# Reordering the attention of the last four batches: value corrections ahead of the key and query corrections, odd chunks' keys turned one chunk early, and the choice of tokens in two steps

## The chip, the cores and the metric

The kernel runs on one core of a Trainium2 chip. The metric is device time in microseconds (us) from one launch. All data are float32. Five engines work side by side from queues of their own: TensorE (PE in the profile; PEld are its weight loads), VectorE (DVE), ScalarE (ACT), GpSimd (POOL) and SyncE (SP), which here only issues DMAs. TensorE writes to PSUM, the others copy results from there to SBUF.

## The reference

A layer of the macaron kind on x of shape 8 x 1024 x 512: half of an expert FFN, attention, half of the same expert FFN, each on the layer-normed x and added to it.

```python
x = x + 0.5 * ffn(layernorm(x), gate_w, gate_b, w1, w2)
x = x + attn(layernorm(x), Wq, bq, Wk, bk, Wv, bv, Wo, bo)
x = x + 0.5 * ffn(layernorm(x), gate_w, gate_b, w1, w2)

# attn, 16 heads of 32, linear and causal
q, k = exp(x @ Wq.T + bq), exp(x @ Wk.T + bk); v = x @ Wv.T + bv
kv = cumsum(k[..., :, None] * v[..., None, :]); k1 = cumsum(k)
out = (q @ kv) / sum(q * k1); out = out @ Wo.T + bo

# ffn: 32 experts, each chooses 8 tokens of each batch
probs = softmax(x @ gate_w.T + gate_b, over tokens)
vals, idx = top_k(probs.T, 8)
merged = sum over the 8 of x[idx] * vals                # one row per expert
o = gelu(merged @ w1 + b1) @ w2 + b2
out[idx] += o * vals
```

## The kernel before

The kernel has four stages, which show in the trace: the choice for the first FFN (to about 145 us), the first FFN (to about 815 us), attention (to about 1930 us) and the second FFN. Both FFNs stream 256 blocks of 2 MB of expert weights through TensorE.

The first FFN is bound by that stream, so a generator `speculate` runs beside it and projects the centred x of batches 4 to 7 with Wq, Wk and Wv. Queries, keys and values of each pair of chunks are stored in DRAM (`ahead_d`). They are projections of x before the FFN's output is added. In attention such a batch is only corrected: the FFN's output for a batch is a sum of 32 expert rows, so the correction is a matmul of 32 rows with the projected expert rows (`oW` for q and k, `oWv` for v), scaled by the tokens' 1/sigma.

Attention takes the 8 batches in turn, each in 8 chunks of 128 tokens. Two chunks make a unit. Batches 0 to 3 are projected in place (`project`), batches 4 to 7 come from `project_rest`, a generator with four steps:

- A (L627 to L658): ask for the next unit's `pre`, add the output bias to x (GpSimd), broadcast 1/sigma with two matmuls (`ps_rs`), copy it (`rsb`), multiply it into the chosen probabilities (`pmr`) and into the loaded projections `pre` (GpSimd, two of 128x1024)
- B (L660 to L682): 16 matmuls `ps_qk` (in fours of 32 rows) into the PSUM tiles `sp0` and `sp1`; VectorE adds them to `pre` (`un`, L676, two of 128x1024); ScalarE takes eight exponentials (L679)
- C (L684 to L706): two matmuls `ps_v`; VectorE scales and adds (`va`, L697, two)
- D (L707 to L709): running sums of the keys (`sum_keys`, four scans, L720) and their product with the queries (`times_keys`, GpSimd, L731)

One chunk c of batch b, in the loop of `attention`: `scores` (32 matmuls into `sp0` and `sp1`, masked by VectorE at L788 and by ScalarE and GpSimd at L793 and L795 into `am`), in even chunks `denominators` and step A, then `turn_keys` (four transposes `ps_kt`, copied to `kc` by ScalarE), `project_out` of the chunk before (`ps_o`, L891, with an add and the statistics on VectorE), `spread_denominators` (`ps_rr`), and `attend` (`ps_n`, scaled to `at` at L862, and the running state `ps_kv`). Beside these run two more generators. `begin` adds the FFN's output to the next batch's x (`ps_sc`, `scatter_two`, two VectorE adds and their statistics), four steps and a square root at the end of the fourth. `route` makes the second FFN's choice of the batch before: `ps_rsT`; `ps_rs` with the logits `lg` (L400); `choose` (L404: eight largest values, their indices, the others marked, exponential, product); `ps_pmT`; `ps_m`; `ps_mT`. One step is taken in each chunk.

In the code before, a unit is advanced so, where `rest` says that the unit being prepared is one of batches 4 to 7: A in the even chunk, B behind `attend` of the even chunk, then at the head of the odd chunk `turn_keys`, C and a step of `route`, and only then that chunk's `scores`; D behind `project_out` of the odd chunk, after a step of `begin`.

The pool of PSUM tiles `mm` has three banks, shared by every `ps_` tile named here apart from `sp0`, `sp1` (two banks each, used by `scores`, `ps_qk` and `ps_rr` in turn) and `ps_kv`. Within an engine a scheduler orders the instructions from the program's order and readiness as it is built; on the chip each engine follows that order.

Of the kernel before, what the change touches and what calls it, by code (L numbers as in the profile page):

```python
# [8 lines left out]
F32 = mybir.dt.float32  # L9
AF = mybir.ActivationFunctionType  # L10
ALU = mybir.AluOpType
# [9 lines left out]
def kernel(  # L21
# [382 lines left out]
    def choose(t, lg, rows, g, name, listed=False, el=None):  # L404


        top = t.p2.tile([P, 8], F32, tag="top", name=f"top_{name}")
        nc.vector.max(top[rows, :], lg[rows, :])
        pinned = el is not None
        sm = t.p2.tile([P, 3], F32, tag="sm", name=f"sm_{name}")  # L410
        nc.vector.tensor_scalar_mul(sm[rows, 0:1], top[rows, 0:1], -1.0)
        rest = pm[:, g, :]
        nc.vector.match_replace(rest[rows, :], top[rows, :], lg[rows, :], -1.0e30)
        if listed and not pinned:
            nc.vector.max_index(chosen_idx[rows, g, :], top[rows, :], lg[rows, :])
        el = el if pinned else lg
        nc.scalar.activation(
            el[rows, :], lg[rows, :], AF.Exp, bias=sm[rows, 0:1], accum_out=sm[rows, 1:2]
        )
        kept = nc.vector.scalar_tensor_tensor(  # L420
            rest[rows, :], rest[rows, :], -0.9e30, el[rows, :], ALU.is_lt, ALU.mult
        )
        if pinned:
            tc.keep_in_program_order(kept)
        nc.vector.reciprocal(sm[rows, 2:3], sm[rows, 1:2])
        if pinned:
            return rest, sm[rows, 2:3], top
        return rest, sm[rows, 2:3]

    def gather_four(t, xs, rs4, chosen, r, g):  # L430

# [48 lines left out]
    def route(t, s, b, el=None):  # L480

        g = b // 4
        own = slice(32 * (b % 4), 32 * (b % 4) + E)
        rows = own
        xt = s["xt", b][0]
        mv = s["mv", b]
        lg = t.p1.tile([P, S], F32, tag="lg", name=f"lg_{b}")
        sd = t.small.tile([P, NCH], F32, tag="sd", name=f"sd_g{b}")  # L490
        rs = t.small.tile([P, NCH], F32, tag="rs", name=f"rs_g{b}")
        at = 0
        for k in (NCH,) if el is None else (4, 2, 1, 1):
            cols = slice(at, at + k)
            nc.scalar.activation(sd[:, cols], mv[:, cols, 1], AF.Sqrt, bias=eps_t)
            if el is not None and at + k == NCH:

                junk = t.small.tile([P, 1], F32, tag="junk", name="junk")
                tc.keep_in_program_order(nc.scalar.activation(junk, eps_t, AF.Exp))
            nc.vector.reciprocal(rs[:, cols], sd[:, cols])  # L500
            for _ in gate_scale(t, s, b, lg, rs, at, k):
                if el is None:
                    yield
            at += k
            if at < NCH:
                yield
        if el is None:
            yield
        chosen, r, *top = choose(t, lg, rows, g, f"b{b}", True, el)
        diag = t.p2.tile([P, E], F32, tag="diag", name=f"diag_{b}")  # L510
        scaled = nc.vector.tensor_scalar_mul(diag[rows, :], ident[rows, rows], r)
        if el is not None:
            tc.keep_in_program_order(scaled)
            tc.keep_in_program_order(
                nc.vector.max_index(chosen_idx[rows, g, :], top[0][rows, :], lg[rows, :])
            )
        if el is None:
            yield

        pmT = t.p1.tile([P, NCH, E], F32, tag="pmT", name=f"pmT_{b}")  # L520
        ps = t.mm.tile([P, NCH, E], F32, tag="mm", name=f"ps_pmT_{b}")
        for c in range(NCH):
            nc.tensor.matmul(
                ps[:, c, :],
                lhsT=chosen[rows, c * P : (c + 1) * P],
                rhs=diag[rows, :],
                start=True,
                stop=True,
            )
# [32 lines left out]
        if el is None:  # L562
            yield
        ps = t.mm.tile([P, NDC, E], F32, tag="mm", name=f"ps_mT_{b}")
        for dc in range(NDC):
            nc.tensor.matmul(
                ps[:, dc, :], lhsT=m[:, dc * P : (dc + 1) * P], rhs=isum, start=True, stop=True
            )
        nc.vector.tensor_copy(mT[:, :, :, b], ps)
        if el is None:  # L570
            yield
# [51 lines left out]
    def project_rest(t, s, b, u):  # L623
# [33 lines left out]
            load_ahead(t, s, *divmod(b * (NCH // U) + u + 1, NCH // U))  # L657
        yield  # L658

        qkT = open_unit(t, s, b, u)  # L660
        sp = [
            t.sc.tile([P, 2, 2, UT], F32, tag=f"sp{h}", name=f"ps_qk{h}_{b}_{u}") for h in range(2)
# [14 lines left out]
        for n, bias in ((1, bk_sb), (0, bq_sb)):  # L677
            for oc in range(NDC):
                nc.scalar.activation(  # L679
                    qkT[:, oc, n, :], qkT[:, oc, n, :], AF.Exp, bias=bias[:, oc : oc + 1]  # L680
                )
        yield  # L682

        ps = [t.mm.tile([P, D], F32, tag="mm", name=f"ps_v_{b}_{u * U + i}") for i in range(U)]  # L684
        for i in range(U):
            r = slice(E * ((b + i) % 4), E * ((b + i) % 4 + 1))
            nc.tensor.matmul(
                ps[i],
                lhsT=pmr[r, i * P : (i + 1) * P],
                rhs=s["oWv", i][r, :],  # L690
                start=True,
                stop=True,
            )
        for i in range(U):
            c = u * U + i
            va = t.a2.tile([P, D], F32, tag="va", bufs=3, name=f"va_{b}_{c}")
            nc.vector.scalar_tensor_tensor(  # L697
                va,
                pre[:, (2 * NDC + i * 2) * UT : (2 * NDC + i * 2 + 2) * UT],
                rs[:, c : c + 1],  # L700
                ps[i],
                ALU.mult,
                ALU.add,
            )
            s["va", b, c] = va
        yield  # L706
        sum_keys(t, s, b, u)  # L707
        times_keys(t, s, b, u)
# [241 lines left out]
    def attention(t, early, preload):  # L950
# [44 lines left out]
        for _ in begun:  # L995
            pass
        last = None
        for b in range(B):
            for c in range(NCH):
                if c == 0:  # L1000
# [22 lines left out]
                if b == B - 1 and c == NCH - 2:  # L1023
# [4 lines left out]
                    el = end.enter_context(tc.tile_pool(name="el", bufs=1, side="right")).tile(  # L1028
                        [P, S], F32, name="el"
                    )  # L1030
                    gate = route(t, s, b, el)
                if rest and c % U:
                    turn_keys(t, s, b, c)
                    next(ahead)
                    next(gate, None)
                scores(t, s, b, c)
                if c % U == 0:
                    denominators(t, s, b, c // U)
# [23 lines left out]
                    values(t, s, b, c)  # L1062
                if not (rest and c % U):
                    turn_keys(t, s, b, c)
                if last is not None:
                    project_out(t, s, *last)
                    if c == 0:
                        for h in range(2):
                            store_x(out, s["xt", b - 1][0], b - 1, h)
                        gate_sums(t, s, b - 1, range(NCH // 2, NCH))  # L1070
                        gate = route(t, s, b - 1)
                    if c == NCH // 2:
                        gate_sums(t, s, b, range(c))
                    if b == B - 1 and c == NCH - 2:
                        gate_sums(t, s, b, range(NCH // 2, c))
                    if b == B - 1 and c == NCH // 2:
                        store_x(out, s["xt", b][0], b, 0)
                if c % U == 0:
                    spread_denominators(t, s, b, c // U)
                else:  # L1080
                    if rest and c > 1:
                        next(begun, None)
                    next(ahead, None)
                if not (rest and c % U):
                    next(gate, None)
                if (b, c) == (0, 1):
                    outputs_turned(t, s, 0)
                attend(t, s, b, c)
                if rest and c % U == 0:
                    next(ahead)  # L1090
                last = (b, c)
        gate_sums(t, s, B - 1, range(NCH - 2, NCH - 1))
# [576 lines left out]
```

## Time and profile before

| what | value |
|---|---|
| median of 3 runs | 2604.76 us (2601.95 to 2608.11) |
| profiled execution | 2606.22 us, span of its core 2604.5 us |
| mean granted TensorE clock | 0.915 |
| busy: TensorE, VectorE, ScalarE, GpSimd | 2190.8, 862.3, 500.4, 376.6 us |
| chain that ended last | TensorE 50%, issue 23%, DMA 16%, VectorE 5% |
| attention, batches 0 to 3 (830 to 1498 us) | TensorE busy 653.97 of 668 us, clock 0.99 |
| batch 4 (1518.4 to 1623.9 us) | TensorE busy 98.19 of 105.5 us, clock 0.92, VectorE 77.75 |
| batch 5 (1623.9 to 1730 us) | TensorE busy 99.45 of 106.1 us, clock 0.90, VectorE 77.23 |
| batch 6 (1730 to 1836 us) | TensorE busy 98.65 of 106 us, clock 0.92, VectorE 78.19 |
| second FFN (1900 to 2604 us) | TensorE busy 426.7 of 704 us, DMA share 0.93 |

A row of the timeline gives start, length, engine, source line, operation, output<-inputs, shape and count; in square brackets the idle time before it and what released it. Float32 matmuls are counted twice or more in the profile[...]. The busy time of a matmul at half clock is longer than at full clock, so busy time and the clock belong together. The profiled execution is 1.5 us above the median.

### The profile page before, as it was taken

The numbers are of one execution on the slowest core, as the hardware profiler recorded it, in microseconds if no ns is written. First come the engines' busy times: TensorE is split into PE (matmuls) and PEld (weight loads), VectorE is DVE, ScalarE is ACT, GpSimd is POOL, SyncE is SP. The second block draws the span as 40 slices with busy tenths as digits, with TensorE's granted clock in tenths as the row PEclk, the third lists the DMA queues.
The fourth block names the chain that finished last, engine by engine and source line by source line (L and its number), as shares of the span: only waits on it lengthen the run. The fifth ranks groups of instructions, "written<-read, shape, count | busy, mean of one in ns | idle before, by whom it ended". The sixth has DMA issues, their size and how long they took to land.

```text
span 2604.5 us, 41783 instructions
## 1 busy us (share of the span) xinstructions
PE 2190.8 (84%) x18679; PEld 1153.6 (44%) x18679; DVE 862.3 (33%) x1495; ACT 500.4 (19%) x965; POOL 376.6 (14%) x345
## 2 busy tenths in 40 slices
PE   8799999898986999999999989999986565555555
PEld 5354545444533666666666655555551111101111
DVE  6411111111102443444534466777750000100002
ACT  6310000000000322222223243343430000000000
POOL 0000000000000212111122145545324000000002
PEclk9999999999998999999999989989888878777788
DMA  7799999999996000010100233333159999999995
GB/s 276 305 426 427 427 427 427 426 427 428 427 429 255 1 18 1 21 50 20 52 9 19 79 110 124 106 113 109 68 210 389 425 427 428 428 428 428 428 427 239
DMA packets 95635, 668.22 MB, mean 257 GB/s; under 512 B 18254, under 2 KB 22606, under 8 KB 58592
## 3 DMA queue, kind: packets, MB, share of 16 engines
q1 hardware_dynamic: 73952, 621.71, 58.1%
q10 hardware_dynamic: 18432, 35.66, 3.5%
q0 software_dynamic: 3072, 8.19, 0.8%
q8 instruction: 146, 2.39, 0.4%
q14 instruction: 33, 0.27, 0.0%
HBM read 614.34 MB, written 48.23 MB: 254 GB/s over the span
## 4 chain that ended last, share of the span: by engine, by line
PE 50%; issue 23%; DMA 16%; DVE 5%; ACT 2%; POOL 1%; SPq 0%; POOLq 0%; ACTq 0%; DVEq 0%
DMA w<-in_w 11%; PE ps_o L891 8%; PE ps_k L603 4%; PE ps_q L603 4%; PE ps_v L811 4%; PE ps_sk L1143 3%; PE ps_sq L1143 3%; PE p_ps L1256 3%; PE h_ps L1233 3%; PE ps_n L841 2%; PE sp L777 2%; PE ps_n L853 2%; PE ps_sv L1160 2%; DMA xg<-out,chosen_idx 2%; PE ps_sc L293 1%
## 5 line engine op out<-in xcount | busy, mean ns | idle before, releaser
L1233 PE MATMUL h_ps<-w,mT 128*8 128x512 f32 x2048 | 294.4, 703 | 126.2 <-DMA w<-in_w 124.3
L1242 DVE STREAM_TRANSPOSE hs<-h_ps 128x512 f32<-128x512 f32 x64 | 45.9, 717 | 721.6 <-PE h_ps L1233 716.3
L1256 PE MATMUL p_ps<-w,pm 128*32 128x512 f32 x1024 | 168.9, 790 | 130.3 <-DMA w<-in_w 122.0
L891 PE MATMUL ps_o<-wo_sb,at 128*128 128x512 f32 x512 | 258.5, 652 | 0.2
L1233 PEld LDWEIGHTS h_ps<-w,mT 128*8 128x8 f32 x2048 | 51.2, 95 | 342.4 <-issue 208.7
L1256 PE MATMUL p_ps<-w,gl 128*32 128x512 f32 x1024 | 133.5, 654 | 38.6 <-DMA w<-in_w 38.3
L594 POOL TENSOR_TENSOR xt<-xt,bo_sb 128x512 f32<-128x512 f32 x32 | 45.8, 1447 | 763.1 <-PE ps_ocT L338 703.4
L1256 PEld LDWEIGHTS p_ps<-w,pm 128*32 128x32 f32 x1024 | 36.0, 127 | 265.7 <-issue 136.5
L891 PEld LDWEIGHTS ps_o<-wo_sb,at 128*128 128x128 f32 x512 | 102.0, 210 | 115.0 <-issue 110.0
L795 POOL TENSOR_SCALAR_AFFINE_SELECT am<-am 128x512 f32<-128x512 f32 x128 | 79.0, 642 | 398.7 <-ACT am L793 260.8
L314 DVE BATCH_NORM_STATS2 st<-xt 128x6 f32<-128x512 f32 x192 | 128.4, 684 | 5.1 <-DMA xt<-in_x 2.5
L603 PE MATMUL ps_k<-xnT,wk_sb 128*128 128x256 f32 x512 | 115.3, 383 | 10.8 <-ACT xnT L339 10.8
L1249 ACT ACTIVATE pm<-a 128x128 f32<-128x128 f32 x32 | 9.9, 309 | 586.5 <-DVE a L1244 580.5
L1143 PE MATMUL ps_sq<-xcT,wq_sb 128*128 128x256 f32 x512 | 118.7, 388 | 4.1 <-ACT xcT L241 4.1
L1143 PE MATMUL ps_sk<-xcT,wk_sb 128*128 128x256 f32 x512 | 117.4, 385 | 0.0
L1160 PE MATMUL ps_sv<-wv_sb,xcT 128*128 128x512 f32 x256 | 115.6, 599 | 0.0
L811 PE MATMUL ps_v<-wv_sb,xnT 128*128 128x512 f32 x256 | 115.1, 593 | 0.0
L603 PE MATMUL ps_q<-xnT,wq_sb 128*128 128x256 f32 x512 | 115.1, 382 | 0.0
L1143 PEld LDWEIGHTS ps_sq<-xcT,wq_sb 128*128 128x128 f32 x512 | 96.8, 193 | 35.3 <-issue 17.4
L1143 PEld LDWEIGHTS ps_sk<-xcT,wk_sb 128*128 128x128 f32 x512 | 96.8, 192 | 27.6 <-issue 15.0
L603 PEld LDWEIGHTS ps_k<-xnT,wk_sb 128*128 128x128 f32 x512 | 95.8, 190 | 28.6 <-ACT xnT L339 14.7
L777 PE MATMUL sp<-un 32*128 32x128 f32 x2048 | 104.8, 302 | 3.9 <-DVE un L676 3.8
(246 smaller groups left out, 2846.3 us busy)
## 6 DMA issues: line engine op xcount, KB each, us to landing
w<-in_w SPq DMA_DIRECT2D x256, 2048.0 KB, 29.8
xt<-in_x SPq DMA_DIRECT2D x31, 1024.0 KB, 10.8
pre<-ahead_d SPq DMA_DIRECT2D x16, 1536.0 KB, 6.5
ahead_d<-ahead_qk ACTq DMA_DIRECT2D x16, 1024.0 KB, 11.5
out<-xt SPq DMA_DIRECT2D x16, 1024.0 KB, 5.4
xs<-in_x ACTq DMA_DIRECT2D x16, 512.0 KB, 19.7
ahead_d<-ahead_v ACTq DMA_DIRECT2D x16, 512.0 KB, 11.0
pm<-pm SPq DMA_DIRECT2D x16, 128.0 KB, 2.5
```

The source lines that it names most:

```text
L314: nc.vector.bn_stats(st, xt[:, c, :])
L603: nc.tensor.matmul(ps[:, o, :], lhsT=w_sb[n][:, dc, oc * P : (oc + 1) * P], rhs=xnT[:, dc, :], start=(dc == 0), stop=(dc == NDC - 1),)
L777: nc.tensor.matmul(sp[r // 2][:, r % 2, og, :], lhsT=kT[hr, og, cols], rhs=qT[hr, og, cols], start=True, stop=True,)
L795: nc.gpsimd.affine_select(out=am[1][:, i, :, :], in_=am[1][:, i, :, :], pattern=[[0, NDC], [1, P]], compare_op=ALU.is_ge, fill=0.0, base=0 ...
L811: nc.tensor.matmul(ps, lhsT=s["xnT", b, c // U][:, dc, cols], rhs=w_sb["v"][:, dc, :], start=(dc == 0), stop=(dc == NDC - 1),)
L841: nc.tensor.matmul(ps[hr, og, :], lhsT=va[:, (og * HG + r) * HD : (og * HG + r + 1) * HD], rhs=am[r // 2][:, r % 2, og, :], start=(og == 0 ...
L853: nc.tensor.matmul(ps[hr, og, :], lhsT=kv[hr, og, :], rhs=qT[hr, og, cols], start=False, stop=True, skip_group_check=True,)
L891: nc.tensor.matmul(ps, lhsT=at[:, oc, :], rhs=w_sb["o"][:, oc, :], start=(oc == 0), stop=(oc == NDC - 1),)
L1143: nc.tensor.matmul(ps[:, o, :], lhsT=w_sb[w][:, dc, oc * P : (oc + 1) * P], rhs=xcT[:, dc, :], start=(dc == 0), stop=(dc == NDC - 1),)
L1160: nc.tensor.matmul(ps, lhsT=xcT[:, dc, i * P : (i + 1) * P], rhs=w_sb["v"][:, dc, :], start=(dc == 0), stop=(dc == NDC - 1),)
L1233: nc.tensor.matmul(h[32 * j : 32 * j + B, :], lhsT=mT[:, dc, e, :], rhs=w1h[dc // 2][:, dc % 2, j * 512 : (j + 1) * 512], start=(dc == 0), ...
L1256: nc.tensor.matmul(pp[32 * j : 32 * (j + 1), :], lhsT=gl4[e % 4][:, q, :, :].rearrange("p i b -> p (i b)"), rhs=w2h[q // (NU // 2)][:, q % ...
```

## The change

Four things change, all in the loop of `attention` and the generators it drives.

1. In `project_rest` the correction of the values (`ps_v`, `va`) comes before that of queries and keys (`ps_qk`, `un`, exponentials).
2. In the even chunk (other than 6) the odd chunk's `turn_keys` and both corrections follow `attend`. The odd chunk's head then has only the step of `route`, the step of `begin` (which was behind `project_out`) and `scores`. In chunk 7 the values are corrected behind `scores` and the rest behind `project_out`; running sums follow at the head of the next batch's chunk 0.
3. In chunk 0 of batches 4 to 7 `project_out` of the batch before, its stores, `gate_sums` and the new `route` come ahead of `scores`. They are gathered in a function `finish_chunk`.
4. `choose` is split: `choosing` yields between the indices of the eight largest and the rest, so `route` has one step more; the indices are taken before the others are marked. All rest of `route` is finished before the last batch's own `route` begins.

```diff
+        if listed and in_place:
+            nc.vector.max_index(chosen_idx[rows, g, :], top[rows, :], lg[rows, :])
+            yield None
         nc.vector.match_replace(rest[rows, :], top[rows, :], lg[rows, :], -1.0e30)
-        if listed and not pinned:
-            nc.vector.max_index(chosen_idx[rows, g, :], top[rows, :], lg[rows, :])
...
@@ def project_rest
         yield
+        ps = [t.mm.tile([P, D], F32, tag="mm", name=f"ps_v_{b}_{u * U + i}") for i in range(U)]
...
+            s["va", b, c] = va
+        yield
         qkT = open_unit(t, s, b, u)
...
                 nc.scalar.activation(
                     qkT[:, oc, n, :], qkT[:, oc, n, :], AF.Exp, bias=bias[:, oc : oc + 1]
                 )
-        yield
-        ps = [t.mm.tile([P, D], F32, tag="mm", name=f"ps_v_{b}_{u * U + i}") for i in range(U)]
...
-            s["va", b, c] = va
         yield
         sum_keys(t, s, b, u)
@@ def attention
+        def finish_chunk(b, c):
+            nonlocal gate
+            project_out(t, s, *last)
+            if c == 0:
+                for h in range(2):
+                    store_x(out, s["xt", b - 1][0], b - 1, h)
+                gate_sums(t, s, b - 1, range(NCH // 2, NCH))
+                gate = route(t, s, b - 1)
+            if c == NCH // 2:
+                gate_sums(t, s, b, range(c))
...
+                    for _ in gate:
+                        pass
                     gate = route(t, s, b, el)
-                if rest and c % U:
-                    turn_keys(t, s, b, c)
+                if c == 0 and b >= NB0:
+                    finish_chunk(b, c)
                     next(ahead)
+                if rest and c % U and c < NCH - 1:
                     next(gate, None)
+                    if c > 1:
+                        next(begun, None)
                 scores(t, s, b, c)
...
-                if last is not None:
-                    project_out(t, s, *last)
...
+                if rest and c == NCH - 1:
+                    next(ahead)
+                if last is not None and not (c == 0 and b >= NB0):
+                    finish_chunk(b, c)
                 if c % U == 0:
                     spread_denominators(t, s, b, c // U)
                 else:
-                    if rest and c > 1:
-                        next(begun, None)
                     next(ahead, None)
...
                 attend(t, s, b, c)
-                if rest and c % U == 0:
+                if rest and c % U == 0 and c < NCH - 2:
+                    turn_keys(t, s, b, c + 1)
+                    next(ahead)
                     next(ahead)
```

More of the change, by code (lines that the diff above doesn't have):

```diff
@@ L404, in choose, with choosing @@
     def choose(t, lg, rows, g, name, listed=False, el=None):
+        *_, made = choosing(t, lg, rows, g, name, listed, el)
+        return made
+    def choosing(t, lg, rows, g, name, listed, el=None):
         top = t.p2.tile([P, 8], F32, tag="top", name=f"top_{name}")
         nc.vector.max(top[rows, :], lg[rows, :])
-        pinned = el is not None
         sm = t.p2.tile([P, 3], F32, tag="sm", name=f"sm_{name}")
@@ L412, in choose @@
         rest = pm[:, g, :]
+        in_place = el is None
+        if listed and in_place:
+            nc.vector.max_index(chosen_idx[rows, g, :], top[rows, :], lg[rows, :])
+            yield None
         nc.vector.match_replace(rest[rows, :], top[rows, :], lg[rows, :], -1.0e30)
-        if listed and not pinned:
-            nc.vector.max_index(chosen_idx[rows, g, :], top[rows, :], lg[rows, :])
-        el = el if pinned else lg
+        el = lg if in_place else el
         nc.scalar.activation(
@@ L422, in choose @@
         )
-        if pinned:
+        if not in_place:
             tc.keep_in_program_order(kept)
         nc.vector.reciprocal(sm[rows, 2:3], sm[rows, 1:2])
-        if pinned:
-            return rest, sm[rows, 2:3], top
-        return rest, sm[rows, 2:3]
+        yield (rest, sm[rows, 2:3]) if in_place else (rest, sm[rows, 2:3], top)
     def gather_four(t, xs, rs4, chosen, r, g):
@@ L508, in route @@
             yield
-        chosen, r, *top = choose(t, lg, rows, g, f"b{b}", True, el)
+        for made in choosing(t, lg, rows, g, f"b{b}", True, el):
+            if made is None:
+                yield
+        chosen, r, *top = made
         diag = t.p2.tile([P, E], F32, tag="diag", name=f"diag_{b}")
@@ L658, in project_rest @@
         yield
+        ps = [t.mm.tile([P, D], F32, tag="mm", name=f"ps_v_{b}_{u * U + i}") for i in range(U)]
+        for i in range(U):
+            r = slice(E * ((b + i) % 4), E * ((b + i) % 4 + 1))
+            nc.tensor.matmul(
+                ps[i],
+                lhsT=pmr[r, i * P : (i + 1) * P],
+                rhs=s["oWv", i][r, :],
+                start=True,
+                stop=True,
+            )
+        for i in range(U):
+            c = u * U + i
+            va = t.a2.tile([P, D], F32, tag="va", bufs=3, name=f"va_{b}_{c}")
+            nc.vector.scalar_tensor_tensor(
+                va,
+                pre[:, (2 * NDC + i * 2) * UT : (2 * NDC + i * 2 + 2) * UT],
+                rs[:, c : c + 1],
+                ps[i],
+                ALU.mult,
+                ALU.add,
+            )
+            s["va", b, c] = va
+        yield
         qkT = open_unit(t, s, b, u)
@@ L681, in project_rest @@
                 )
-        yield
-        ps = [t.mm.tile([P, D], F32, tag="mm", name=f"ps_v_{b}_{u * U + i}") for i in range(U)]
[L685 to L704, printed above, removed]
-            s["va", b, c] = va
         yield
@@ L997, in attention @@
         last = None
+        def finish_chunk(b, c):
[8 more added lines that the diff above has]
+                gate_sums(t, s, b, range(c))
+            if b == B - 1 and c == NCH - 2:
+                gate_sums(t, s, b, range(NCH // 2, c))
+            if b == B - 1 and c == NCH // 2:
+                store_x(out, s["xt", b][0], b, 0)
         for b in range(B):
@@ L1064, in attention @@
                     turn_keys(t, s, b, c)
-                if last is not None:
-                    project_out(t, s, *last)
[L1067 to L1077, printed above, removed]
+                if rest and c == NCH - 1:
+                    next(ahead)
+                if last is not None and not (c == 0 and b >= NB0):
+                    finish_chunk(b, c)
                 if c % U == 0:
```

## The prediction

> **What bounds the kernel now.** I read the stretches of the trace first (columns: start and end, length, then busy microseconds of TensorE, its weight loads, VectorE, ScalarE and GpSimd with counts, the granted clock, the DMA share, GB/s):
>
> ```profile
> 830.00:1498.00 668.00, 653.97 (x6359) 441.67 (x6347) 301.26 (x477) 181.99 (x334) 129.32 (x116) 0.99 0.08 27
> 1623.90:1730.00 106.10, 99.45 (x1361) 59.82 (x1357) 77.23 (x120) 41.75 (x80) 50.30 (x40) 0.90 0.31 108
> 1900.00:2604.00 704.00, 426.70 (x2723) 102.56 (x2721) 83.72 (x155) 30.23 (x72) 53.35 (x57) 0.80 0.93 391
> ```
>
> The first row is attention of the batches projected in place: TensorE full, clock 0.99. The last is the second FFN, bound by its weight stream, so whatever attention gains or loses moves it one for one. The middle row is one of the batches 4 to 7, the only ones the change rearranges: 106 us, TensorE 6.6 us idle and at clock 0.90. The waits of TensorE over these batches (1518 to 1905 us) name the idle time, in the columns total, times, longest:
>
> ```profile
> PE ps_rs L388 <- DVE va L697: 5.2, 4, 1.3
> PE ps_pmT L523 <- DVE va L697: 5.2, 4, 1.3
> PE ps_mT L566 <- DVE va L697: 5.2, 4, 1.3
> PE sp L777 <- DVE un L676: 3.5, 6, 0.6
> ```
>
> So in odd chunks a step of the choice needs a PSUM bank that the correction of the values releases late. The timeline of chunk 3 of batch 5, and the clock in half-microsecond slices, show what it costs:
>
> ```profile
> 1659.31 1.15 PE L667 MATMUL ps_qk<-pmr,oW 32*128 32x256 f32 x16
> 1660.39 0.66 PE L827 MATMUL ps_kt<-ident,un 128*128 128x128 f32 x4
> 1660.98 1.13 PE L687 MATMUL ps_v<-oWv,pmr 32*128 32x512 f32 x4
> 1663.62 2.92 PE L523 MATMUL ps_pmT<-diag,pm 32*128 32x32 f32 x13 [1.30 <-DVE va L697]
> ...
> 1668.55 4.67 PE L891 MATMUL ps_o<-wo_sb,at 128*128 128x512 f32 x8
> ```
> ```profile
> 1663.00:1663.50 0.50, 0.00 (x0) 0.00 (x0) 0.50 (x2) 0.50 (x3) 0.00 (x0) 1.00 0.00 0
> ...
> 1664.00:1664.50 0.50, 0.50 (x4) 0.50 (x4) 0.50 (x2) 0.50 (x2) 0.00 (x0) 0.50 0.00 0
> ...
> 1670.00:1670.50 0.50, 0.50 (x2) 0.08 (x1) 0.50 (x1) 0.00 (x0) 0.50 (x1) 0.50 0.90 203
> 1671.00:1671.50 0.50, 0.50 (x3) 0.26 (x2) 0.00 (x0) 0.00 (x0) 0.50 (x1) 1.00 0.23 35
> ```
>
> The reader is to see 1.3 us of idle, then half clock from 1663.6 to 1670.5. In batch 5 such drops last about 3.5 us in chunks 1 and 7 and 6.9 us in chunks 3 and 5: 20.8 us at half rate, so 10.4 us lost, beside 5 us of idle (three gaps of 1.3 and chunk 7's). Of the 16 odd chunks of these batches all but the last, in which no unit is projected, show the drop (ps_o takes 4.7 to 5.9 us there, 3.7 in even chunks). This is what a new order could win: 15 us a batch at most.
>
> **The rule and the row.** The Trainium skill ("TensorE: Matmul & The Clock Gate", section "HAM oscillation") says that idle gaps above some 3.4 us throttle the array. The row above differs: 1.3 us is enough here, and in chunk 7 two gaps of 0.51 and 0.64. I take the row; the sum is also made by the rule, with no drop after gaps under 3.4 us.
>
> **The change, step by step.** No matmul, DMA or activation is added or removed in a unit; the choice in batches 0 to 3 only shifts by a chunk, under TensorE's 654 of 668 us, so 0 (if the cover were gone, the 14 us idle in that row bounds it). The built order on each engine gives the rest. I lay a batch out in six sections between marks read in batch 5's timeline, with durations of the trace: scores 1.1, ps_v 1.0, ps_qk 1.1, ps_kt 0.6, ps_o 3.6, ps_lg 1.5, ps_n 2.0, ps_kv 0.4; VectorE: va pair 1.40, un pair 2.36, a scan 0.65, a scatter add 0.66, statistics 0.69, am 1.2, at 0.69; ScalarE: eight exponentials 3.5, four lg 2.1, am 1.0; GpSimd: am pair 1.23, qk 2.36.
>
> 1. *End of ps_kv of chunk 6 to the next batch's scores.* Before 1610.90 to 1623.90, 13.0. After: scores 1.1, ps_v 1.0, ps_o 3.6, ps_qk 1.1, to 6.8. On VectorE the add and statistics of that ps_o (1.6) now stand before the un pair, which ends at 9.7, and `at` of chunk 7 behind it at 10.4. ps_n ended at 8.8, and ps_o of chunk 7 is now next: a new idle of 1.7. ps_o and ps_lg make 15.6, or 17.3 with a drop of one window (3.4 us at half, 1.7 lost).
> 2. *To the end of ps_n of chunk 0.* Before 10.3 (to 1634.16), with the ps_o and ps_lg that went into 1. After: scores 1.1; then am copied and masked (1.0 + 1.2), against ps_den, ps_rs, ps_kt beside it; rr waits for am and the 1.75 us reciprocal. 5.4. Sections 1 and 2: 23.3 before, 21.0 to 22.7 after.
> 3. *To ps_rr of chunk 1.* Before 22.1 (1656.27). The un pair ended 3.6 after the start; now ps_kt, ps_v and the va pair go first and it ends at 6.0. The exponentials then end at 8.7, the lg activations at 10.8 (8.6 before), and VectorE's maximum waits for them. From there to the reciprocal that releases ps_rr VectorE is full for 13.0 us (1643.25 to 1656.23). So 24.1: putting the values first delays the choice by 2 us. TensorE is idle 1.6 before ps_rr.
> 4. *To ps_rr of chunk 2.* Before 29.0 (1685.29), with the double drop above. After: ps_n to ps_qk ends at 5.7, the scatter fills 1.05, scores wait until the un pair ends at 8.65 (1.9 idle), end 9.8, ps_o 13.4; am at 14.3, as two scatter adds, statistics and two scans precede it; then ps_n, scatter, scores, ps_den to ps_kt, ps_o, ps_lg: 25.7. pmT (1.3) has moved on to 5. With one drop and part of another 27.2.
> 5. *To ps_rr of chunk 3.* Before 28.6 (1713.91). After, pmT, ps_n, ps_kv, ps_kt to 5.0, ps_v, ps_qk, ps_m 1.7 and the scatter cover the un pair: scores from 10.0 to 11.1 with no stall, the best point of the change. But ps_o takes a bank that the first scatter add releases, and this stands behind two scans and the statistics of ps_m: 12.9 to 16.5. And ps_n of chunk 5 needs am, whose mask on GpSimd is queued behind qk, which needs the fourth scan: VectorE runs without pause from 6.2 to 18.4 (va 1.4, un 2.4, scans, ps_m's three steps, two scatter adds, statistics, am), qk ends at 20.9, the masks at 22.1. ScalarE adds to it: the square root of the next batch, with a 1.28 us table load, now stands before the copy of am. TensorE idle about 5 us. ps_n, ps_kv, scores, ps_den, ps_rs, ps_kt and ps_o then give 30.8, or 32.5 with a drop.
> 6. *To the end of ps_kv of chunk 6.* Before 3.05, after 3.95 (ps_mT, 0.9, moved here).
>
> Sums: 106.1 before; after 105.5 without drops under the rule, 110.4 with them. In all 15 of those chunks idle of 1.15 us or more is followed by a drop, and the new gaps are as long; so I take 109.5, the nearer to the row: +3.4. This holds for batches 4 to 6, +10.3. Batch 7 has no next batch, so no scatter, square root or statistics: section 3 costs 1.0 instead of 2.0, section 4 gains 1.1, the others cancel, about 0 (-3.0 to +1.7). The first unit (chunks 6 and 7 of batch 3) waited 6.57 us for pmr; scores now go before this wait and part of the tail shifts: -1.6. SP's queue has one swap: `pre` of the second unit goes ahead of the next x loads, which wait for ps_m, now a chunk later. `pre` lands in 6.5 us (table of DMA issues) and is used some 20 later, x in 10.8 us and is used a batch's third, some 35 us, later: nothing; without that cover it would be the chunk, 13 us.
>
> Total +8.7: 2606.2 + 8.7 = 2614.9 for the profiled execution's own time; the median of the runs is 1.5 lower than this execution, so **2614**. Ends of the costs: three batches at -0.6 or +4.3, batch 7 at -3.0 or +1.7, the first unit -1.6: -6 to +13, 2598 to 2618 about the median; an unseen wait of 1 us in each of the 12 units with a scatter adds 12 more at the top.
>
> **Rivals.**
> - *The drops go, and the kernel is faster.* If TensorE's fillers (the first ps_o matmul in chunk 1, the scatter in chunks 3 and 5, ps_m) hold the clock at 1.00, and the mask in section 5 isn't kept waiting so long (28.0 there), a batch takes 102.7: 3 x -3.4, -3.0, -1.6 make -15, **2590**. For it: idle of 0.57 before ps_rs and of 0.5 before ps_rr left the clock at 1.00, and chunk 5 gets its scores without stall. Against: VectorE needs 5.0 us from the start of ps_v to the end of the un pair, TensorE has 2.1 plus 0.9 to 1.05 of filler in chunks 1 and 3.
> - *Give and take, no difference.* The double drops become single ones (-3.4 a batch in chunks 3 and 5) and pay exactly for section 3 and a shorter wait in 5: **2605**. For it: the work is the same. Against: VectorE's 12 us row in section 5.
> - *The wait behind GpSimd is worse.* Each chunk 5 stays at half clock for two windows and section 3 gets a drop: +6 a batch, **2622**. It is my forecast's own mechanism at its top.
> - *The order is undone by the scheduler.* Excluded: the built order has the values first.
>
> **Chances.** Forecast (2607 to 2619) 0.45, worse 0.15, no difference 0.17, faster 0.23. What a measurement here can tell from no change is about 0.2%, 5 us. Slower: 0.58, as a little of the forecast lies within 5 us; same 0.18; faster 0.24. Range: from 2590 to 2628.
>
> **What would show it.** Right: TensorE's long wait in chunks 5 of batches 4 to 6 is ps_n for GpSimd's mask, with half clock behind it; the wait for va is gone, in its place scores wait for the un pair in chunks 1 and 3; ps_o of chunk 7 waits for `at` about 1.7 us; a batch takes 108 to 111 us, batch 7 about as before. Wrong: a granted clock near 1.00 from 1518 us on, or batches under 105 us; then VectorE's queue was less full than its summed rows.

## The result: 0.76% slower, and the profile after

The changed kernel takes 2625.03 us in the median of 6 runs (2618.85 to 2632.76), the kernel before 2606.19 beside it: ratio 1.0076, 95% interval 1.0059 to 1.0093. The profiled execution has a span of 2623.4 us against 2604.5, mean granted clock 0.923 against 0.915.

The same three stretches as before, in the same columns (start and end, length, busy time of TensorE, its weight loads, VectorE, ScalarE, GpSimd, then clock, DMA share, GB/s); the second is batch 5 between the same marks, the third is moved by the 19 us that the end moved:

```profile
830.00:1498.00 668.00, 652.75 (x6372) 441.94 (x6367) 302.01 (x478) 181.97 (x333) 129.56 (x117) 0.99 0.09 28
1619.28:1728.50 109.22, 97.63 (x1367) 58.98 (x1361) 81.75 (x121) 42.25 (x81) 52.45 (x40) 0.94 0.30 105
1919.00:2623.00 704.00, 415.03 (x2728) 98.57 (x2720) 84.09 (x156) 29.43 (x70) 53.24 (x57) 0.81 0.93 392
```

Batches 0 to 3 and the second FFN are as before. Batch 5 has a better clock (0.94 for 0.90) and yet is longer: TensorE is idle for 11.6 us instead of 6.6. The waits of TensorE from 1495 to 1930 us (total, times, longest) name the new idle time:

```profile
PE ps_n L848 <- POOL am L802: 18.6, 11, 3.3
PE sp L784 <- DVE un L707: 6.3, 13, 0.7
PE ps_v L670 <- POOL pmr L658: 5.2, 1, 5.2
PE ps_o L898 <- DVE at L869: 4.9, 4, 1.5
PE ps_o L898 <- DVE xt L308: 4.2, 3, 1.4
PE ps_n L848 <- DVE am L795: 3.9, 4, 1.2
PE ps_v L670 <- DVE xt L905: 3.6, 2, 1.8
```

The three waits for `va` (15.6 us in all) are gone. In their place the product `ps_n` waits for the mask on GpSimd, 18.6 us, up to 3.3 at a time. Chunk 3 of batch 5, shown before with a gap of 1.30 us and ps_o at half speed behind it, has only short gaps now, yet a shorter drop:

```profile
1670.86 0.37 PE L698 MATMUL ps_qk<-pmr,oW 32*128 32x256 f32 x1
...
1672.34 0.49 PE L784 MATMUL sp<-un 32*128 32x128 f32 x4 [0.25 <-DVE un L707]
1673.47 1.57 PE L784 MATMUL sp<-un 32*128 32x128 f32 x28 [0.64 <-DVE un L707]
1674.97 4.93 PE L898 MATMUL ps_o<-wo_sb,at 128*128 128x512 f32 x8
```

The loss is two chunks on, in chunk 5. First TensorE, then what GpSimd, ScalarE and VectorE did meanwhile, from the timeline of the changed kernel:

```profile
1703.72 3.70 PE L898 MATMUL ps_o<-wo_sb,at 128*128 128x512 f32 x8 [1.39 <-DVE xt L308]
1708.66 0.41 PE L848 MATMUL ps_n<-am,va 128*32 128x128 f32 x4 [1.23 <-DVE am L795]
1712.41 2.50 PE L848 MATMUL ps_n<-am,va 128*32 128x128 f32 x28 [3.35 <-POOL am L802]
```
```profile
1705.61 2.87 POOL L643 TENSOR_TENSOR xt<-xt,bo_sb 128x512 f32<-128x512 f32 x2 [11.56 <-DVE st L314]
1707.53 0.30 ACT L988 ACTIVATE sd<-mv,eps_t 128x8 f32<-128x8 f32 x1 [2.90 <-DVE mv L315]
1707.73 0.99 ACT L800 COPY am<-sp 128x1024 f32<-128x1024 f32 x1
1709.43 2.34 POOL L738 TENSOR_TENSOR qk<-un 128x1024 f32<-128x1024 f32 x1 [0.95 <-DVE rs L989]
1711.73 1.22 POOL L802 TENSOR_SCALAR_AFFINE_SELECT am<-am 128x512 f32<-128x512 f32 x2
1708.52 0.74 DVE L727 TENSOR_TENSOR_SCAN un<-ones,un,un 128x256 f32<-128x256 f32 x1
```

The copy of `am` is there at 1708.72, but GpSimd masks it at 1711.73: qk stands ahead in its queue and itself waits for the fourth scan (VectorE, the last row above; the profile names the short reciprocal `rs` right behind it, which qk does not read). The copy was late too: the scores were done at 1702.34, and the square root, ahead on ScalarE, waited for statistics until 1707.53. The clock in half-microsecond slices of the same place (the clock is the third number from the right):

```profile
1711.00:1711.50 0.50, 0.00 (x0) 0.00 (x0) 0.00 (x0) 0.00 (x0) 0.50 (x1) 1.00 1.04 397
1711.50:1712.00 0.50, 0.00 (x0) 0.00 (x0) 0.00 (x0) 0.00 (x0) 0.50 (x2) 0.61 1.02 385
1712.50:1713.00 0.50, 0.50 (x2) 0.10 (x3) 0.00 (x0) 0.00 (x0) 0.45 (x1) 0.50 0.10 37
...
1718.00:1718.50 0.50, 0.50 (x20) 0.50 (x19) 0.00 (x0) 0.00 (x0) 0.00 (x0) 0.56 0.00 0
1718.50:1719.00 0.50, 0.50 (x24) 0.38 (x20) 0.00 (x0) 0.00 (x0) 0.00 (x0) 1.00 0.00 0
```

After 4.6 us of idle in two pieces comes half clock for 6.8 us. To place the loss, the stretch from ps_rr in chunk 6 of batch 3 to ps_rr in chunk 6 of batch 7 is cut at every ps_rr (chunks 0, 2, 4, 6; the prediction's sections number the last three by their unit, 1 to 3), and like sections of the four batches are added (us):

| section | before | after |
|---|---|---|
| chunk 7 of batch 3 with the first unit, to chunk 0 of batch 4 | 31.5 | 33.3 |
| the other three around a chunk 7 | 71.7 | 70.5 |
| four around chunk 1 | 98.2 | 101.8 |
| four around chunk 3 | 111.6 | 110.6 |
| four around chunk 5 | 113.2 | 129.5 |
| sum | 426.2 | 445.7 |

16.3 of the 19.5 us are around chunk 5 (+4.6, +4.7, +5.3 in batches 4 to 6, +1.7 in batch 7). In the whole stretch TensorE's idle time rose from 32.6 to 54.2 us, while the time at half clock fell from 85.3 us (in 16 runs) to 61.4 (12). Priced at half their length, these give +21.6 and -12: the change won clock and paid more in waits. The two don't close to +19.5. Some 10 us stay unassigned: TensorE's busy time, with the part at half clock counted half, is itself 9 us more after the change (363 us for 354) for the same matmuls, and why isn't shown.

### The profile page after: what moved, and what is told of

Its sections match the earlier page's. It is cut to its first block, busy times and chain, and to the rows that moved or that the text cites. A ratio compares the mean times of both kernels' runs of the same rounds, so it can differ in the third digit from the quotient of the medians.

```text
span 2623.4 us, 41809 instructions
## 1 busy us (share of the span) xinstructions
PE 2173.9 (83%) x18679; PEld 1151.0 (44%) x18679; DVE 881.9 (34%) x1495; ACT 502.3 (19%) x965; POOL 383.0 (15%) x345
## 4 chain that ended last, share of the span: by engine, by line
PE 48%; issue 22%; DMA 16%; DVE 6%; POOL 2%; ACT 2%; POOLq 0%; ACTq 0%; DVEq 0%; SPq 0%
DMA w<-in_w 13%; PE ps_o L898 7%; PE ps_k L610 4%; PE ps_q L610 4%; PE ps_v L818 4%; PE ps_sk L1164 3%; PE ps_sq L1164 3%; PE ps_n L848 2%; PE h_ps L1254 2%; PE p_ps L1277 2%; PE sp L784 2%; PE ps_n L860 2%; DMA xg<-out,chosen_idx 2%; PE ps_sv L1181 2%; DVE un L707 1%
## 5 line engine op out<-in xcount | busy, mean ns | idle before, releaser
L1254 PE MATMUL h_ps<-w,mT 128*8 128x512 f32 x2048 | 283.9, 688 | 121.6 <-DMA w<-in_w 121.0
L898 PE MATMUL ps_o<-wo_sb,at 128*128 128x512 f32 x512 | 241.5, 614 | 9.9 <-DVE at L869 4.9
L898 PEld LDWEIGHTS ps_o<-wo_sb,at 128*128 128x128 f32 x512 | 94.4, 195 | 115.2 <-issue 100.3
L1164 PEld LDWEIGHTS ps_sq<-xcT,wq_sb 128*128 128x128 f32 x512 | 95.4, 190 | 32.7 <-issue 15.3
## 6 DMA issues: line engine op xcount, KB each, us to landing
xt<-in_x SPq DMA_DIRECT2D x31, 1024.0 KB, 11.6
```

Of the source, the lines that this page charges most:

```text
L898: nc.tensor.matmul(ps, lhsT=at[:, oc, :], rhs=w_sb["o"][:, oc, :], start=(oc == 0), stop=(oc == NDC - 1),)
L1164: nc.tensor.matmul(ps[:, o, :], lhsT=w_sb[w][:, dc, oc * P : (oc + 1) * P], rhs=xcT[:, dc, :], start=(dc == 0), stop=(dc == NDC - 1),)
L1254: nc.tensor.matmul(h[32 * j : 32 * j + B, :], lhsT=mT[:, dc, e, :], rhs=w1h[dc // 2][:, dc % 2, j * 512 : (j + 1) * 512], start=(dc == 0), ...
```

## Experiments

The theory: chunk 5's queues (VectorE's, and behind it ScalarE's and GpSimd's) hold up `am`. The rivals: the values ahead of the keys cost by themselves; the choice split into two steps; the work put ahead in chunk 0. All ratios are to the kernel before in the same series of runs (medians of before 2604.6 to 2609.3). Sections, idle time and half clock come from the one profiled execution of each kernel; it lies within 4 us of the median, except in the swap of the mask (7 us below it) and in the second mix (6 above).

**Undo one part of the change each.** The step of the next batch goes back behind `project_out`:

```diff
                 if rest and c % U and c < NCH - 1:
                     next(gate, None)
-                    if c > 1:
-                        next(begun, None)
...
                 else:
+                    if rest and c > 1:
+                        next(begun, None)
                     next(ahead, None)
```

> The changed kernel with the step of begin in odd chunks put back behind project_out; all else as changed. Queue theory (the cost sits in chunk 5, where scatter adds, statistics and the square root stand ahead of the scans and of the copy of am, so the mask on GpSimd ends late): am and its mask in chunk 5 end about 16 us after ps_rr of chunk 2 instead of 21, ps_rr of chunk 3 comes 4 to 6 us earlier in batches 4 to 6, in all 10 to 18 us less than the changed kernel, 2607 to 2615. Values-first theory (the cost is that the corrections of q and k come 2 us later): chunk 5 keeps its wait for another reason, within 3 us of the changed kernel.

Measured 2612.82 us, ratio 1.0031 (1.0017 to 1.0045), 12 less than the changed kernel. The sections around chunk 5 went from 129.5 to 117.8 us, the others by at most 0.8. So two adds, statistics and a square root in front of `am` are a large part of the loss.

Keys before values again, the rest as changed:

```diff
@@ project_rest
+        qkT = open_unit(t, s, b, u)
...
+        yield
+
         ps = [t.mm.tile([P, D], F32, tag="mm", name=f"ps_v_{b}_{u * U + i}") for i in range(U)]
...
             s["va", b, c] = va
         yield
-        qkT = open_unit(t, s, b, u)
...
-        yield
         sum_keys(t, s, b, u)
```

> The changed kernel with the correction of queries and keys ahead of that of the values again, both still behind the even chunk. Values-first theory: the un pair ends 1.5 to 2.4 us earlier in every unit, the lg activations and the maximum too, and at of chunk 7 no longer stands behind it: 3 to 4 us a batch, 12 to 16 us less than the changed kernel. Queue theory: the chain of VectorE in chunk 5 is as long as before and starts at the same time, since va only changes place with un; 0 to 6 us less (section 3 only).

Measured 2620.1, ratio 1.0061 (1.0048 to 1.0074), 5 less than changed. Chunk 5 stays at 128.2, so the order isn't the main cause. It is give and take: the first unit gains 5.8 us (27.5), the sections around chunks 1 and 3 gain 4.5 and 3.2, but the three around chunk 7 lose 9.9 (80.4 for 70.5).

`project_out`, stores, sums and the new `route` of chunk 0 back at their old place:

```diff
                 if c == 0 and b >= NB0:
-                    finish_chunk(b, c)
                     next(ahead)
...
-                if last is not None and not (c == 0 and b >= NB0):
+                if last is not None:
                     finish_chunk(b, c)
```

> The changed kernel with project_out, stores, gate sums and the new route of chunk 0 put back behind turn_keys; the running sums stay ahead of scores. By the sections of the trace (kv of chunk 6 to ps_n of chunk 0 took 20.6 us instead of 23.3 in batch 5) this part of the change gained 2.6 us a batch, so undoing it costs 6 to 11 us: 2631 to 2636. If the gain came from moving the corrections in chunk 7 instead, undoing it changes nothing or gains up to 1.5 us a batch, the idle time of ps_o of chunk 7 for at.

Measured 2648.32, ratio 1.0175 (1.0161 to 1.0188): 23 more than changed, twice the expected top. The sections around chunk 7 rose to 83.4 and the first unit to 36.8. TensorE now waits for qk before `ps_den` (9.8 us) and for the exponentials before `scores` (8.5): with the correction begun only in chunk 7, the early ps_o and logits are what covers it.

The choice in one step:

```diff
-        for made in choosing(t, lg, rows, g, f"b{b}", True, el):
-            if made is None:
-                yield
-        chosen, r, *top = made
+        *_, made = choosing(t, lg, rows, g, f"b{b}", True, el)
+        chosen, r, *top = made
```

> The changed kernel with the choice made in one step again, so ps_pmT, ps_m and ps_mT come one chunk earlier. Queue theory: the three VectorE steps of ps_m (1.6 us) leave the chain of chunk 5, and chunk 4 has room for them: 1 to 2 us a batch, 3 to 8 us less than the changed kernel. Clock theory (the loss is in the drops, and these follow the low-activity matmuls of the choice): ps_pmT after the stall of chunk 3 doubles the drop there again, 2 us a batch more, 6 to 8 us more than the changed kernel.

Measured 2624.28, ratio 1.0077 (1.0064 to 1.0091): no difference to the changed kernel. Neither side was right: chunk 5 gains 5.5 us (124.0), chunk 3 loses 6.4 (117.0).

**Do one part alone on the kernel before.** Only `project_out`, stores, sums and route of chunk 0 ahead of `scores` (`finish_chunk` as in the change, put on the kernel before):

```diff
+                if c == 0 and b >= NB0:
+                    finish_chunk(b, c)
                 if rest and c % U:
...
-                if last is not None:
-                    project_out(t, s, *last)
...
+                if last is not None and not (c == 0 and b >= NB0):
+                    finish_chunk(b, c)
```

> The kernel before with one part of the change alone: project_out of chunk 7, the stores, the gate's sums and the new route ahead of chunk 0's scores in batches 4 to 7, nothing else. If this part is good by itself, as 23 us lost without it in the changed kernel suggest: 2585 to 2600. If it only repays a wait that the values' new place makes (scores of chunk 0 waiting for the exponentials): 2603 to 2613, since one piece of TensorE's work is only put ahead of another.

Measured 2615.59, ratio 1.0025 (1.0018 to 1.0033): a loss of 6.3 against the 2609.33 of its series. It is good only where a later correction needs covering, as the rival of that expectation said, though 2615.59 lies above its range too. Only the choice in two steps (with `choosing` as in the change):

```diff
-        chosen, r, *top = choose(t, lg, rows, g, f"b{b}", True, el)
+        for made in choosing(t, lg, rows, g, f"b{b}", True, el):
+            if made is None:
+                yield
+        chosen, r, *top = made
```

> The kernel before with one other part alone: the choice in two steps, a chunk apart. The half clock of chunk 3 behind ps_pmT's 1.3 us wait should go from two windows to one and come up again in chunk 5. If chunk 5's VectorE queue is what decides, the later steps of the choice make it longer there and the sum is +1 to +5 (2606 to 2610); if the wait for the bank is what decides, a batch gains 1.7 to 3 us (2595 to 2600).

Measured 2594.72, ratio 0.9945 (0.9931 to 0.9959): 14 us faster by itself, as much as the wait for the bank promised and not what VectorE's queue in chunk 5 did. Its sections around chunk 3 are 102.2 us against 111.6, around chunk 5 106.6 against 113.2, its half clock 37.5 us against 85.3. In chunk 3 no step of the choice waits for `va` any more. The wait is still there in chunks 1 and 5 (before ps_rs and ps_m, eight times 1.3 us), but in chunk 5 it is ps_m that follows it, matmuls of 128x512, instead of ps_mT with its 128x32 pieces. In the changed kernel no such wait was left to be relieved; the split brought nothing there.

**Mixes.** Both start from the kernel with the next batch's step put back. `correct_values` and `correct_keys` are the two blocks of `project_rest` as functions; the second mix differs from the first, shown here, in the condition `u or b == NB0`:

```diff
-            if made is None:
+            if made is None and b != B - 2:
                 yield
...
+        steps = (correct_values, correct_keys)
+        for step in steps[::-1] if (b, u) == (NB0, 0) else steps:
+            step()
+            yield
```

> The run with the next batch's step back behind project_out (2612.8), and with two things more: the first unit alone corrects its keys before its values, and the choice that runs beside batch 7 is made in one step. If what the single runs showed adds up: the first unit's 5.8 us (27.5 against 33.4 from its chunk 7's ps_rr to the next) and about 3.5 us in chunk 5 of batch 7 (26.1 against 29.1 to 29.8) come off, 2602 to 2605, no difference to before. If these were shifts that are given back in the next chunk, 2609 to 2614.

> As the mix before it, but keys before values in every unit except the one of chunk 0 of batches 5 to 7, where the values' correction goes ahead of the scores. If the loss by keys first (3.3 us from chunk 7 to the next batch's chunk 0) comes only from that unit and the gains in chunks 1 to 4 (1 to 2 us a batch) from the others: 2596 to 2602, faster than before. If the gains of keys first in chunks 1 to 4 come from the unit of chunk 0 itself: 2603 to 2610.

2603.97 (0.998, 0.9973 to 0.9987) and 2589.59 (0.9925, 0.991 to 0.994): the gains of single sections add up in the first, and the second is better than its range and beats the kernel before (its sections around chunk 3 are 104.8 us for the first mix's 113.1, with 27.3 us of half clock in all). Of that, 9.5 us come off in batches 4 and 6 and 0.3 in batch 5, while batch 7 gives 1.6 back: a wait that only batches 4 and 6 had is gone, described below under what was mis-sized.

**The mask itself.** The sharpest test leaves the order of every engine but GpSimd as it is in the changed kernel; there, the product qk goes behind the mask of the same chunk, in chunks 1, 3 and 5 (in chunk 7 the changed kernel has the mask ahead of qk already):

```diff
         sum_keys(t, s, b, u)
+        yield
         times_keys(t, s, b, u)
...
-        nc.gpsimd.tensor_mul(qk, s["q", b, u], s["k1", b, u])
+        made = nc.gpsimd.tensor_mul(qk, s["q", b, u], s["k1", b, u])
+        if b >= NB0:
+            tc.keep_in_program_order(made)
...
                     finish_chunk(b, c)
+                    next(ahead)
                     next(ahead)
...
                 attend(t, s, b, c)
+                if rest and c % U and c < NCH - 1:
+                    next(ahead)
```

> The changed kernel with one swap on GpSimd's queue: in the batches projected beside the first FFN the product qk of a unit's correction stands behind the mask of that chunk's am instead of ahead of it; the order on all other engines is the same. If the mask behind qk is the wait that decides in chunk 5 (the copy of am is done at 1708.72 of the changed kernel's trace, the masks begin at 1711.73): 3 us off in chunks 5 of batches 4 to 6 and 1 to 2 elsewhere, 2611 to 2617 against 2625. If VectorE's queue decides by itself (what else stands in it must be done before the next product or ps_o anyway) and the mask is only the last in line: 2620 to 2626. If denominators that now come late take its place: above 2626.

Measured 2605.98, ratio 1.0005 (0.9994 to 1.0016): 19 us off the changed kernel by one swap, more than expected, and level with the kernel before. The sections around chunk 5 are 112.6 us, for 129.5 in the changed kernel and 113.2 before. The same place in its timeline:

```profile
1702.69 0.41 PE L851 MATMUL ps_n<-am,va 128*32 128x128 f32 x4 [1.23 <-DVE am L798]
1702.84 1.48 POOL L805 TENSOR_SCALAR_AFFINE_SELECT am<-am 128x512 f32<-128x512 f32 x2 [0.32 <-ACT am L803]
1703.78 0.41 PE L851 MATMUL ps_n<-am,va 128*32 128x128 f32 x2 [0.67 <-POOL am L805]
1704.28 2.35 POOL L739 TENSOR_TENSOR qk<-un 128x1024 f32<-128x1024 f32 x1
1704.37 1.06 PE L851 MATMUL ps_n<-am,va 128*32 128x128 f32 x26 [0.18 <-POOL am L805]
1705.36 1.08 PE L863 MATMUL ps_n<-un,kv 32*32 32x128 f32 x32
```

The wait of 3.35 has become 0.67 and 0.18, qk follows the mask, and the clock holds: the rows from ps_rr to ps_rr of this chunk, in the changed kernel and in this one,

```profile
1691.00:1724.30 33.30, 27.31 (x362) 16.59 (x358) 18.58 (x30) 10.32 (x20) 13.48 (x11) 0.90 0.47 160
```
```profile
1685.00:1713.20 28.20, 24.71 (x360) 14.79 (x356) 18.61 (x30) 10.31 (x20) 13.77 (x11) 1.00 0.56 189
```

show 2.5 us less idle and 2.6 less busy time for the same matmuls, VectorE as full as ever (18.6 us). So VectorE's queue is not the bound by itself; it makes qk late, and qk blocks the mask.

A control on the kernel before, with the same edit to `project_rest` and `times_keys` and a step behind `attend` in every odd chunk (`if rest and c % U: next(ahead)`):

> A control: the kernel before with the same swap on GpSimd's queue alone (qk behind the mask, all other engines in the same order). If the wait for the masks is something that the change brings about, as the kernel before's list of waits says (ps_n for the mask there 1.5 us in all, at most 0.2 each), nothing changes: within 3 us of before. If the swap is good in itself, whatever stands around it: 8 to 19 us less, and the change compared with it would be a loss of 10 us or more still.

Measured 2595.29, ratio 0.9964 (0.9952 to 0.9977): 9 us faster. The expectation of no change fell, as did the idea that the list of waits (1.5 us for the mask there) bounds what a swap can bring. Idle time is the same (32.7 us for 32.6), but half clock falls from 85.3 to 71.7 us. Chunk 3 of batch 5 shows how; the gap is the one of before, to the hundredth:

```profile
1661.97 1.63 PE L523 MATMUL ps_pmT<-diag,pm 32*128 32x32 f32 x13 [1.30 <-DVE va L697]
...
1664.62 5.40 PE L894 MATMUL ps_o<-wo_sb,at 128*128 128x512 f32 x8
```

Here half clock begins 3.0 us after the end of the gap, not with it (1665.0), so that ps_pmT runs at full clock, and lasts 3.4 us, not 6.8. But most of the control's gain is elsewhere: 6.1 us in the three sections around chunk 7 (65.6 for 71.7), where the changed kernel has the mask ahead of qk without the swap, and 1.5 each around chunks 3 and 5. So the wait around chunk 5 is the change's own: the change adds 16.3 us there, the swap takes 16.9 off the changed kernel and 1.5 off the kernel before.

With the swap in both, the change still costs 10.7 us by the medians. Of the 7.6 between the two traces +2.3 is in the first unit, +5.1 around chunk 7 (where ps_o waits up to 1.5 us for `at`), +2.2 around chunk 1, -2.9 and +0.9 around chunks 3 and 5.

**The best order found.** Chunks 1 to 5 as in the kernel before with the split choice, chunks 7 and 0 as changed; then with the swap on GpSimd. The first keeps the edits of the second mix (keys first but for the unit of chunk 0, the choice beside batch 7 in one step, the next batch's step back) and adds:

```diff
                 if rest and c % U and c < NCH - 1:
+                    turn_keys(t, s, b, c)
+                    next(ahead)
                     next(gate, None)
...
                 if rest and c % U == 0 and c < NCH - 2:
-                    turn_keys(t, s, b, c + 1)
-                    next(ahead)
                     next(ahead)
```

> A mix of the two fastest: chunks 1 to 5 in the order of the kernel before with the choice in two steps (keys before values, the values' correction and the choice at the head of the odd chunk), chunks 7 and 0 in the changed kernel's order (values first, project_out ahead of the scores). From the sections between ps_rr's of those two: 27.6 for the first unit, then 25.9, 25.4 and 26.2, and 23.5, 24.4, 25.4, 26.2 in later batches, 99.5 a batch: 2583 to 2588, the fastest so far. If chunk 0's order shifts its loss into chunk 1 (as it did with keys first): 2592 to 2596.

> The mix before it with the product qk behind the mask on GpSimd's queue, all other engines the same. Where chunk 5 isn't held up by VectorE, masks wait less: if the mask's place costs about 0.5 us in each of the 14 odd and even chunks where ps_n still waits for it, 3 to 6 us less than the mix (2578 to 2584); if the wait then falls on the denominators, no difference or up to 4 us more.

2585.86 (0.9933, 0.9916 to 0.995) and 2573.38 (0.9894, 0.9874 to 0.9913). The last is about 1% faster than the kernel before and beats both; its stretch is 399.5 us against 426.2 and 445.7, with 34.4 us idle and 23.9 at half clock. Its list of waits no longer has the mask at its head. Chunk 5 of batch 5 has a gap of 1.30 us, as it had in the kernel before (first row), but with ps_m behind it instead of ps_mT, and no drop at all:

```profile
1694.36 1.89 PE L566 MATMUL ps_mT<-isum,m 128*128 128x32 f32 x8 [1.30 <-DVE va L697]
```
```profile
1674.33 1.92 PE L550 MATMUL ps_m<-xt,pmT 128*32 128x512 f32 x16 [1.30 <-DVE va L682]
1676.18 1.17 PE L794 MATMUL sp<-un 32*128 32x128 f32 x30
1677.28 3.70 PE L908 MATMUL ps_o<-wo_sb,at 128*128 128x512 f32 x8
```

## Why the prediction was right, and what it sized wrong

*Direction and mechanism.* Slower, by the wait of chunk 5 for GpSimd's mask, behind qk, behind the scans: as forecast, and shown by the swap, which takes 16.9 us off the sections to which the change had added 16.3. The waits for `va` went, `scores` waits for the un pair (6.3 us), ps_o of chunk 7 waits 1.5 us for `at` in three batches (1.7 forecast) and 0.5 in batch 3.

*The size.* +19 us is twice what was forecast. 2625 lies above the ends that were summed from the costs (2598 to 2618) and is right only by the wider range. (2614.9 less 1.5 is also 2613.4, not 2614.)

*Batch 5, section by section.* Forecast 15.6 (without the drop), 5.4, 24.1, 25.7 to 27.2, 30.8 to 32.5, 3.95; measured 15.2, 5.4, 24.75, 26.3, 33.3, 4.06: 109.07 in all against 109.5. The largest miss is section 5, 0.8 above its top. That the sum is so near is in part luck. It had about one window of half clock each in sections 1, 4 and 5; the trace has none in section 1, one in 3 (where none was forecast) and 4, two in 5. Batch 7 was put at no change; between ps_rr of chunk 6 of batch 6 and of batch 7 it is 101.8 us before and 101.9 after.

*What was mis-sized.* The forecast put +3.4 us on each of batches 4 to 6 and -1.6 on the first unit, +8.7. From ps_rr of one chunk 6 to the next they moved by +8.1 (batch 4 with the first unit), +3.0 and +8.4, 19.5 in all. Three terms failed.

The first is the price of half clock in section 5. A drop was priced at one window, 1.7 us; the trace has two windows around chunk 5 in each of batches 4, 5 and 6 (in batch 6 apart), 3.4 us. The idle time was forecast at about 5 us and is 6.0 in batch 5. That is what the third rival named, with 2622: two windows in each chunk 5 and a drop in section 3, which batches 5, 6 and 7 show.

The second is a wait that the working of section 4 doesn't have, because batch 5, from which all was sized, doesn't have it. In batches 4 and 6 ps_v waits 1.78 us for the add behind ps_o (`xt` L905 in the list of waits). On VectorE that add stands behind an add of 32x8 numbers to the chosen indices. Batch 4, then the same instruction in batch 5:

```profile
1552.73 4.67 POOL L662 TENSOR_TENSOR pre<-pre,rsb 128x1024 f32<-128x1024 f32 x2
1552.87 2.25 DVE L541 TENSOR_SCALAR chosen_idx<-chosen_idx 32x8 uint32<-32x8 uint32 x1
1555.04 2.40 DVE L518 TENSOR_SCALAR diag<-ident,sm_b 32x32 f32<-32x32 f32 x1
1557.46 0.69 DVE L905 TENSOR_TENSOR xt<-ps_o,xt 128x512 f32<-128x512 f32 x1
1558.30 1.09 PE L670 MATMUL ps_v<-oWv,pmr 32*128 32x512 f32 x2 [1.78 <-DVE xt L905]
```
```profile
1664.53 0.21 DVE L541 TENSOR_SCALAR chosen_idx<-chosen_idx 32x8 uint32<-32x8 uint32 x1
1664.68 4.67 POOL L662 TENSOR_TENSOR pre<-pre,rsb 128x1024 f32<-128x1024 f32 x2
```

Begun 0.14 us after GpSimd's product of `pre`, the small add takes 2.25 us, until the first of the two products is done; begun 0.15 us before it, 0.21; in the kernel before, with nothing on GpSimd beside it, 0.15 to 0.17. The `diag` behind it takes 2.40 in all three batches, to the end of the second product. The section is 29.2 us in batch 4 (two windows of half clock) and 30.1 in batch 6 (three), 26.3 in batch 5 (one): a loss of 1.6 and 2.5 us against the kernel before, and a gain of 2.7. Of the 14 kernels profiled here, the six that have the slow add in batches 4 and 6 (2.24 to 2.25 us) have this wait of ps_v in both, and the eight others have it nowhere. From the first mix to the second it goes, and the section falls from 31.1 and 30.4 us to 26.0 and 26.0 in those batches, from 26.2 to 25.9 in batch 5. No run changes this alone.

The third is the first unit: -1.6 forecast, -0.7 up to ps_rr of batch 3's chunk 6 and +1.8 from there to the next. With keys first it is 5.8 us shorter; the values' correction in front of the keys, behind 5.2 us of waiting for pmr, was not counted against it.

*The rule and the row.* The row was taken (a gap of 1.3 us is enough) against the Trainium skill's gap above some 3.4 us ("TensorE: Matmul & The Clock Gate", section "HAM oscillation"). The traces side with the row: gaps of 1.3 us are followed by half clock. But the row is no rule either: of six gaps of 1.39 to 1.49 us before ps_o in the changed kernel none was (around the one at 1629.5 us the granted clock is 1.00 from 1625 to 1640 us). Without drops the forecast would have been a gain of 0.6 a batch, the wrong way.

*Where a rival had a point.* "The drops go" came half true: half clock fell by 24 us, and with the mask freed by 58 (27.3 left of 85.3). The gain was there and was paid away, around chunk 5, in one queue.

## What to carry to other kernels

When a step is moved, look not only at the engine that it loads but at what stands behind its last product on a second and a third queue: here one product of 2.3 us ahead of a mask of 1.2 cost up to 3.3 us of TensorE and then the clock. A part of a change can be good alone (the split choice, -14 us) and do nothing beside the others, or bad alone (chunk 0's early output, +6) and needed beside the others (23 us lost without it), so parts are tried in both settings. Size a wait from several batches, not from one: 0.3 us in the start of a small instruction decided here between 0.2 us and 2.2. Where the clock falls in windows, give a wait the ends of no drop and two windows.

## What was not expected of the hardware

Half clock comes in whole windows of about 3.4 us on a fixed grid: in the kernel before it begins at 1534.0, 1561.3, 1588.6, 1615.9, 1639.8 and 1663.7 us, 27.3 or 23.9 apart, 8 or 7 times 3.41, and lasts 3.4, 6.8 or 13.7.

One and the same gap of 1.30 us, in chunk 3 of batch 5, was followed by 6.8 us of half clock in the kernel before and by 3.4 in the control. In the first the gap lies in one window of the grid; in the control the grid, counted from the half clock at 1665.0, splits it into 0.9 and 0.4. This holds for every gap of 1.3 us before ps_pmT in the 14 traces here, 14 gaps in five kernels: the 6 that lie whole in one window are followed by two windows of half clock, the 8 that are split by one.

Whether a drop comes at all goes with what follows the gap. All 14 of these and all 14 such gaps before ps_mT (128x32) have one, but only one of the 10 before ps_m (128x512), though three of these lie whole in one window, and none of the 33 gaps of 1.2 to 1.5 us before ps_o. That small pieces count for little in a window would fit this and the split choice's 48 us less half clock, but it is a reading: the gaps also lie in different chunks, with other work around them, and before ps_rs (8x128 pieces) 10 of 12 have a drop.

The control shows how much hangs on the grid: with the idle time of TensorE the same and the order of every engine but GpSimd as before, it has four windows fewer in the stretch (21 for 25).
